# An attention and gated FFN kernel: content products of queries and keys on row halves, the norm's steps and products on other engines, pools in another order

## The chip, the cores and the metric

One core of a Trainium2 chip. The time is the device time of one execution in microseconds (us), the median of several runs; smaller is better. TensorE (PE) multiplies matrices, VectorE (DVE), ScalarE (ACT) and GpSimd (POOL) work elementwise, and SyncE (SP) issues the DMAs.

## The reference

Everything is fp32. For x of 8 batches, 256 positions and 512 columns, with 128 heads of 4 content columns and 64 rotary columns:

```python
xn = (x - mean(x)) / sqrt(var(x) + 1e-5)
c_q, c_kv = xn @ Wq_down, xn @ Wkv_down              # 512 -> 64 each
q_c, k_c, v_c = c_q @ Wq_up, c_kv @ Wk_up, c_kv @ Wv_up   # 64 -> 128 heads x 4
q_r, k_r = xn @ Wq_rope, xn @ Wk_rope                # 128 heads x 64; one of 64 for all heads
scores = (q_c . k_c + q_r . k_r) / sqrt(68)
s = softmax(scores) @ v_c @ Wo
lin(x, wq, A, B) = x @ tile(wq, 4).T + 0.5 * x @ A.T @ B.T
g = silu(lin2(silu(lin1(xn)) * lin3(xn)))            # 512 -> 1376 -> 512, rank 2
out = x + s * g
```

## The kernel before

**First phase** (`first_phase`, the first 230 us or so). The 2048 rows are four blocks (`tb`) of 512 rows, each of four x tiles of 128 rows. For a block, `norm` takes mean and variance of the four tiles on DVE (L359, L360), adds the epsilon (L365) and makes a first guess of the reciprocal root by integer operations (L368, L370); `norm_rest` refines it in three Newton steps of three small DVE operations (L377, L378, L380) and scales the four tiles (L385). `turn` transposes the tiles on TensorE (xpt, L401), copies them out on ACT and DVE in turn (L404, L406) and sums column chunks for the FFN (L410 to L412). `narrow` (pm) and `down` (pp) are the narrow products: `narrow` gives the rank-2 inputs and the rotary keys, `down` the two latents, 64 rows of queries' and 64 of keys'. `down` also calls `sum_x`, which makes sums of x chunks on POOL (L158) and stores them. Then six steps `u` of the FFN follow: `low` (px and py, L451) and `main` (L463, L464), with silu on ACT (L466) and the product hT on DVE (L468, L471, L472), `fold` on POOL (L486 to L488) and `low_out` (pm, L498) on TensorE. `gate_out` (pf) makes the gate of a block, which is stored to DRAM (L524, L525). The work of the next block is set among these steps by hand: its `norm` at u = 1, its `norm_rest` at u = 2, its `turn` after u = 5. `between` sets other work there: `set_up`, which lays out the weights of the content products by POOL copies, and in the last block the first pieces of the second phase.

**Second phase.** 64 blocks `n` are pairs of a batch `b` and a group of 16 heads `sg`; each is done in two halves. A half issues two `score` groups on TensorE (sc, L672, tiles of 32 rows by 128 columns), the maxima on DVE (nmx, L685), exponentials on ACT (pr, L691), transposes on DVE (pt, L701), and one `Project`: the rotary queries of a later block by seven products in place of eight (q, L173, tiles of 128 rows by 32 columns), for which weights w come from DRAM (L124) and their sums ws from POOL (L136 to L139) or DRAM. In a block's first half come also `weigh` (av, L718, the weighted values of the block before), `gather` (L738), and every other pair of blocks `prepare`: the content queries and keys of 32 heads for one batch (qk, 32 calls in all). The stationary weights there are `wupq_sb`, whose lower 64 rows are zero, and `wupk_sb`, whose upper 64 rows are zero, so that each product over all 128 rows of the latents takes its own half. Eight PSUM banks, handed out in rotation by `bank`, carry all of this.

After the first phase its pools are closed, and `w2p` (for `wo_sb`), `prp`, `tp`, `smp` and `op` are opened where they lay. SP's queue then holds, in this order, the gates' stores, the latents of two batches (`load_act`), 32 loads of Wo (L649) and the loads of w. At the end `give` multiplies the output product by the gate, adds x and stores it.

Each engine works off its own instructions in the order in which the program issues them, and so does the queue of SP.

Of the kernel before, what the change touches and what calls it, by code (L numbers as in the profile page):

```python
# [9 lines left out]
F32 = mybir.dt.float32  # L10
I32 = mybir.dt.int32
AF = mybir.ActivationFunctionType
ALU = mybir.AluOpType
# [3 lines left out]
P = 128  # L17
# [7 lines left out]
TB = 512  # L25
# [12 lines left out]
def mla_ffn_gate_kernel(  # L38
# [25 lines left out]
    const = pool("const", 1)  # L64
    ident = const.tile([P, P], F32, name="ident")
    make_identity(nc, ident)
    wupq_sb = const.tile([P, 4, P], F32, name="wupq_sb")
    wupk_sb = const.tile([P, 4, P], F32, name="wupk_sb")
    wv_sb = const.tile([P, 4, P], F32, name="wv_sb")
    mask_sb = const.tile([P, 8], F32, name="mask_sb")  # L70

# [27 lines left out]
    def bank(name):  # L99
        return ps_all.tile([P, 512], F32, tag="b", name=name)  # L100
# [68 lines left out]
    def on_columns(to, w, x, start, stop):  # L169

        for t in range(4):
            tile_ = slice(32 * t, 32 * t + 32)
            nc.tensor.matmul(to[tile_], w[:, tile_], x, start=start, stop=stop, skip_group_check=True)  # L173
# [65 lines left out]
    def prepare(b, g):  # L239


        qk = bank(f"qk_{b}_{g}")
        on_columns(qk[:, :S], wupq_sb[:, g, :], acts[b][:, 0, :], True, True)
        on_columns(qk[:, S:], wupk_sb[:, g, :], acts[b][:, 0, :], True, True)
        qc = qcp.tile([P, S], F32, tag="qc", name=f"qc_{b}_{g}", bufs=3)
        nc.scalar.copy(qc, qk[:, :S])  # L246
        kc = qcp.tile([P, S], F32, tag="kc", name=f"kc_{b}_{g}", bufs=3)
        nc.scalar.mul(kc, qk[:, S:], QSCALE)
        qks[b, g] = qc, kc

    def spread(n):
# [37 lines left out]
    def first_phase(between):  # L289
# [63 lines left out]
        load_x(1)  # L353

        def norm(tb):
            mv = f2.tile([P, 4, 2], F32, tag="mv", name=f"mv_{tb}")
            for n in range(4):
                s6 = f2.tile([P, 6], F32, tag="st", name=f"st_{tb}_{n}")
                nc.vector.bn_stats(s6, xts[tb][n])  # L359
                nc.vector.bn_aggr(mv[:, n, :], s6)  # L360


            var = mv[:, :, 1]
            ve = f2.tile([P, 4], F32, tag="ve", name=f"ve_{tb}")
            nc.vector.scalar_tensor_tensor(ve, var, EPS, var, ALU.add, ALU.max)  # L365

            i0 = f2.tile([P, 4], I32, tag="i0", name=f"i0_{tb}")
            nc.vector.tensor_single_scalar(i0, ve.bitcast(I32), 1, ALU.logical_shift_right)  # L368
            r0 = f2.tile([P, 4], I32, tag="r0", name=f"r0_{tb}")
            nc.vector.tensor_scalar(r0, i0, -1.0, float(0x5F3759DF), ALU.mult, ALU.add)  # L370
            r0 = r0.bitcast(F32)
            return mv, ve, r0

        def norm_rest(tb, mv, ve, r0):
            e = f2.tile([P, 4], F32, tag="e", name=f"e_{tb}")
            for step in range(3):
                nc.vector.scalar_tensor_tensor(e, r0, -0.5, r0, ALU.mult, ALU.mult)  # L377
                nc.vector.scalar_tensor_tensor(e, e, 1.0, ve, ALU.mult, ALU.mult)  # L378
                rstd = f2.tile([P, 4], F32, tag="rstd", name=f"rstd_{tb}_{step}")
                nc.vector.scalar_tensor_tensor(rstd, e, 1.5, r0, ALU.add, ALU.mult)  # L380
                r0 = rstd
            xns[tb] = []
            for n in range(4):
                xn = xts[tb][n]
                nc.vector.scalar_tensor_tensor(  # L385
                    xn,
                    xn,
                    mv[:, n, 0:1],
                    rstd[:, n : n + 1].to_broadcast([P, D]),
                    ALU.subtract,  # L390
                    ALU.mult,
                )
                xns[tb].append(xn)

        def turn(tb):
            a = f1.tile([P, KT, TB], F32, tag="act1", name=f"act1_{tb}")
# [17 lines left out]

        def over_xn(tb, name, weights):
            ps = bank(f"{name}_{tb}")
            for c in range(KT):
                on_columns(ps, weights[:, c, :], xnT[tb][:, c, :], c == 0, c == KT - 1)
            return ps

        def narrow(tb):
# [116 lines left out]
        for tb in range(NTB):  # L538
            more = tb + 1 < NTB
            for u in range(6):  # L540
                low(tb, u)
                main(tb, u)
                if u in (2, 4):
                    fold(tb, u // 2 - 1)
                    low_out(tb, u // 2 - 1)
                if u == 1 and more:
                    stats = norm(tb + 1)
                if u == 2 and more:
                    norm_rest(tb + 1, *stats)
                if u == 1 and tb + 2 < NTB:  # L550
                    load_x(tb + 2)
                if tb == NTB - 2 and u == 1:
                    between(1)
                if u == 5:
                    fold(tb, 2)
                if not more:
                    between(u + 2)
            if more:
                turn(tb + 1)
                low_out(tb, 2)  # L560
                narrow(tb + 1)
                down(tb + 1)
            else:
                low_out(tb, 2)
            gate_out(tb)
# [5 lines left out]
    def set_up():  # L571
# [5 lines left out]
        nc.sync.dma_start(out=v_raw[64:128, :], in_=w_v)  # L577
        for t in range(4):
            nc.sync.dma_start(out=mask_sb[32 * t : 32 * t + 32, :], in_=kmask[0:32, :])
        nc.gpsimd.memset(wupq_sb[64:128], 0.0)  # L580
        nc.gpsimd.memset(wupk_sb[0:64], 0.0)
        nc.gpsimd.memset(wv_sb[0:64], 0.0)
        up = up_raw.rearrange(
            "l (g h u z j i d) -> l g h u z j i d", g=4, h=2, u=2, z=2, i=2, d=HD
# [2 lines left out]
        for r in range(4):  # L587
            for h in range(2):
                to = slice(32 * r + 16 * h, 32 * r + 16 * h + 16)
                of = up[:, :, h, r % 2, 0, :, r // 2, :]  # L590
                for w_sb, rows in ((wupq_sb, slice(0, 64)), (wupk_sb, slice(64, 128))):
                    nc.gpsimd.tensor_copy(
                        w_sb[rows, :, to].rearrange("l g (j d) -> l g j d", d=HD), of[rows]
                    )
            for t in range(4):
                nc.gpsimd.tensor_copy(
                    wv_sb[64:128, t, :].rearrange("l (s r d) -> l s r d", s=8, d=HD)[:, :, r],
                    vr[64:128, :, r % 2, t, r // 2, :],
                )
# [38 lines left out]
    first_phase(between)  # L638


    w2p = pool("wo", 1)
    wo_sb = w2p.tile([P, KT, D], F32, name="wo_sb")

    wo = w_o.rearrange("(c e u t i d) m -> e u t i d c m", e=2, u=2, t=4, i=2, d=HD)
    for r in range(4):
        for t in range(4):
            for e in range(2):
                p = 32 * r + 8 * t + 4 * e
                nc.sync.dma_start(out=wo_sb[p : p + 4], in_=wo[e, r % 2, t, r // 2])  # L649
    prp = pool("pr", 6)  # L650
    tp = pool("pt", 3)
    smp = pool("sm", 2)
    op = pool("out", 2)
    scs, nmxs, prs, pts, accs, outT = {}, {}, {}, {}, {}, {}

    def score(n, f):
# [125 lines left out]
                pos[b, n], outT[b][:, c, ds(n * P, P)], wo_sb[:, c, :], c == 0, c == KT - 1  # L782
            )

    def give(b, n, engine=nc.gpsimd):
        g, xr = gxs.pop((b, n))
        nc.vector.tensor_mul(g, pos[b, n], g)
        engine.tensor_add(g, g, xr)
        nc.sync.dma_start(out=out[ds(b * S + n * P, P), :], in_=g)

    def finish(b, n):
        put(b, n, range(KT))
# [90 lines left out]
    put(B - 1, 1, range(KT))  # L883
    for b in (B - 2, B - 1):
        for i in range(2):
            give(b, i, nc.vector if (b, i) == (B - 1, 1) else nc.gpsimd)


# [64 lines left out]
```

## Time and profile before

| | |
|---|---|
| median of 3 runs | 2027.2 us (2026.76 to 2027.53) |
| profiled execution | 2026.23 us, its span 2024.5 us |
| granted TensorE clock, mean | 0.999 |
| busy: TensorE, DVE, ACT, POOL | 99%, 76%, 53%, 36% of the span |
| HBM read and written | 145.12 MB and 34.08 MB |

A row of a timeline gives the start in us, the length in us, the engine, the line of the kernel, the operation with its output and inputs by the program's names, the shapes, the count, and in brackets how long the engine stood idle before it and what released it. Rows of one kind that follow each other are merged. PEld is TensorE's loading of weights, SPq the queue of SyncE. A row of the waits gives who waited for whom, the sum in us, how often, and the longest. The ends of TensorE's records are modelled, so starts are what is compared here. One fp32 product leaves two records.

### The profile page before, as it was taken

What the parts mean: (1) busy time and instruction counts of PE and PEld (TensorE: products, weight loads), DVE (VectorE), ACT (ScalarE), POOL (GpSimd) and SP (SyncE); (2) the same over time, 40 slices, a digit from 0 to 9 for tenths busy, and PEclk for the clock granted to TensorE, in tenths of its full rate; (3) what the DMA queues carried; (4) which work ended last, traced back from release to release, by engine and by line L of the source; (5) the groups of instructions that cost most, each with busy time, mean ns of one, the idle gap of its engine ahead of it and who ended that gap; (6) DMA issues with size and microseconds to landing.
All of it is one profiled execution on the core that took longest, in us unless ns stands there. A gap on an engine that the chain in (4) does not pass through costs nothing.

```text
span 2024.5 us, 86560 instructions
## 1 busy us (share of the span) xinstructions
PE 2008.1 (99%) x38080; PEld 1417.0 (70%) x38080; DVE 1544.5 (76%) x2638; ACT 1072.4 (53%) x2978; POOL 720.7 (36%) x1044
## 2 busy tenths in 40 slices
PE   8999999999999999999999999999999999999998
PEld 3334477777777776777777777677777767777776
DVE  6542387878798777878787877878787877888788
ACT  1222365565556554556555644555555545556654
POOL 5434445545552323233232233223323223232231
PEclk9999999999999999999999999999999999999999
DMA  5233322222223223322223123222223222222212
GB/s 167 87 113 134 110 97 75 76 86 86 86 75 128 80 91 103 99 86 67 84 86 122 65 105 110 81 82 86 68 90 115 82 100 81 86 85 79 72 55 70
DMA packets 118043, 184.77 MB, mean 91 GB/s; under 512 B 10434, under 2 KB 83810, under 8 KB 117668
## 3 DMA queue, kind: packets, MB, share of 16 engines
q1 hardware_dynamic: 117668, 179.23, 26.0%
q8 instruction: 301, 4.93, 1.0%
q14 instruction: 74, 0.61, 0.1%
HBM read 145.12 MB, written 34.08 MB: 89 GB/s over the span
## 4 chain that ended last, share of the span: by engine, by line
PE 95%; DVE 1%; DMA 0%; issue 0%; ACT 0%; POOL 0%; SPq 0%; DVEq 0%; ACTq 0%
PE q L173 39%; PE sc L672 33%; PE av L718 11%; PE po L173 2%; PE pf L173 2%; PE px L173 2%; PE py L173 1%; PE qk L173 1%; PE px L451 1%; PE vps L270 1%; DVE pt L701 1%; PE pm L173 1%; PE pp L173 1%; PE pm L498 0%; DVE nmx L685 0%
## 5 line engine op out<-in xcount | busy, mean ns | idle before, releaser
L691 ACT ACTIVATE pr<-sc,nmx 128x256 f32<-128x256 f32 x2048 | 816.4, 502 | 476.4 <-DVE nmx L685 470.9
L685 DVE TENSOR_REDUCE nmx<-sc 128x2 f32<-128x512 f32 x1024 | 635.4, 683 | 318.8 <-PE sc L672 293.3
L701 DVE STREAM_TRANSPOSE pt<-pr 128x512 f32<-128x512 f32 x1024 | 634.8, 677 | 0.0
L672 PE MATMUL sc<-act,qr 32*128 32x256 f32 x8192 | 490.1, 374 | 0.1
L173 PE MATMUL q<-x,ws 128*32 128x256 f32 x8192 | 488.8, 379 | 0.1
L216 POOL TENSOR_TENSOR e<-e,e 128x256 f32<-128x256 f32 x128 | 94.0, 734 | 1059.0 <-ACT e L211 557.1
L672 PEld LDWEIGHTS sc<-act,qr 32*128 32x128 f32 x8192 | 422.6, 185 | 21.9 <-issue 0.3
L173 PEld LDWEIGHTS q<-x,ws 128*32 128x32 f32 x8192 | 265.0, 110 | 177.4 <-POOL ws L137 0.6
L173 PE MATMUL q<-x,w 128*32 128x256 f32 x6144 | 381.5, 381 | 1.4 <-ACT pr L691 1.4
L173 PEld LDWEIGHTS q<-x,w 128*32 128x32 f32 x6144 | 186.4, 110 | 155.5 <-ACT pr L691 40.9
L672 PE MATMUL sc<-kc,qcm 32*128 32x256 f32 x4096 | 281.9, 387 | 0.0
L718 PE MATMUL av<-pt,vpad 128*32 128x128 f32 x8192 | 236.4, 273 | 1.9 <-ACT pr L691 1.2
L718 PEld LDWEIGHTS av<-pt,vpad 128*32 128x32 f32 x8192 | 226.3, 110 | 14.5 <-issue 3.0
L672 PEld LDWEIGHTS sc<-kc,qcm 32*128 32x128 f32 x4096 | 199.1, 184 | 52.1 <-issue 38.4
L211 ACT COPY e<-q 128x256 f32<-128x256 f32 x512 | 203.9, 399 | 14.9 <-PE q L173 14.7
L738 ACT ACTIVATE acc<-av,sides_sb 128x256 f32<-128x256 f32 (+1 forms) x130 | 54.2, 468 | 219.2 <-PE av L718 219.2
L255 POOL TENSOR_TENSOR qcm<-qc,mask_sb 128x1024 f32<-128x1024 f32 x64 | 122.2, 1910 | 9.1 <-ACT qc L246 9.1
L217 POOL TENSOR_TENSOR e<-e,e 128x256 f32<-128x256 f32 x128 | 93.6, 731 | 10.0
L218 POOL TENSOR_TENSOR qr<-e,e 128x256 f32<-128x256 f32 x128 | 93.6, 731 | 10.0
L285 POOL COPY vpad<-vall 32x128 f32<-32x128 f32 x256 | 74.8, 292 | 16.0 <-ACT vall L277 5.6
L228 DVE TENSOR_TENSOR qr<-e,q 128x256 f32<-128x256 f32 x128 | 53.9, 421 | 26.2 <-PE q L173 13.6
L468 DVE TENSOR_TENSOR hT<-gate,py 128x512 f32<-128x512 f32 x32 | 21.3, 684 | 65.9 <-PE py L173 39.6
(103 smaller groups left out, 1114.3 us busy)
## 6 DMA issues: line engine op xcount, KB each, us to landing
w<-in_w_rope_dram SPq DMA_DIRECT2D x128, 512.0 KB
ws<-sums_d SPq DMA_DIRECT2D x96, 512.0 KB
sums_d<-ws SPq DMA_DIRECT2D x32, 512.0 KB
x<-xs_d SPq DMA_DIRECT2D x28, 256.0 KB
xt<-in_x_dram SPq DMA_DIRECT2D x16, 256.0 KB
xs_d<-xt SPq DMA_DIRECT2D x16, 256.0 KB
gate_d<-gs SPq DMA_DIRECT2D x16, 256.0 KB
g<-gate_d SPq DMA_DIRECT2D x16, 256.0 KB
```

Of the source, the lines that this page charges most:

```text
L173: nc.tensor.matmul(to[tile_], w[:, tile_], x, start=start, stop=stop, skip_group_check=True)
L211: nc.scalar.copy(self.e[i], self.banks[i])
L216: nc.gpsimd.tensor_add(m6, m6, m1)
L217: nc.gpsimd.tensor_add(m7, m7, m6)
L218: nc.gpsimd.tensor_add(self.out(1, 1), self.split(m7), self.split(m5))
L255: nc.gpsimd.tensor_mul(qcm, qks[b, sg // 2][0].rearrange("p (q i) -> p q i", i=32).unsqueeze(2).to_broadcast([P, 8, 4, 32]), mask_sb[:, ds ...
L285: nc.gpsimd.tensor_copy(vpad[rows, :, :, 8 * t + 4 * (sg % 2) :][..., :4], valls[b][rows, :, sg])
L672: nc.tensor.matmul(sc[r][:, h, :], lhs.rearrange("p t i -> p (t i)"), rhs, start=(part == 0 and h == 0), stop=(part == 2), skip_group_chec ...
L685: nc.vector.tensor_reduce(nmx[:, r, :], scs[n, f][r], AX.X, ALU.max, negate=True)
L691: nc.scalar.activation(p[:, h, :], scs[n, f][r][:, h, :], AF.Exp, bias=nmxs[n, f][:, r, h : h + 1])
L701: nc.vector.transpose(pts[n, f // 2, r].rearrange("p k q i -> p q k i")[:, ds(2 * (f % 2), 2)], prs.pop((n, f, r)).rearrange("p h (k j) -> ...
L718: nc.tensor.matmul(av[32 * r : 32 * r + 32, ds(half * P, P)], vpad[:, k, r, :], pt[r][:, k].rearrange("p q i -> p (q i)"), start=(k == 0), ...
```

## The change

`prepare` multiplies only the 64 rows that matter: the queries' rows 0 to 63 and the keys' rows 64 to 127, each from its own half of one weights tile `wup_sb`, in turn and into two banks. `set_up` fills that tile with half the copies and without zeroing. In `norm` the Newton steps now stand at u = 1; for block 0 they stay on DVE, for the others they run on POOL, which also makes the offset, minus mean times reciprocal root. `norm_rest` stands at u = 4; for block 0 it scales on DVE by `tensor_scalar`, for the others on ACT by one activation per tile. The first `narrow` product of block 0 is made in two halves of its columns. `prp`, `smp` and `op` are opened ahead of `w2p`. The last `give` works in two halves of the columns.

```diff
--- before.py
+++ after.py
@@ -64,8 +64,7 @@
     const = pool("const", 1)
     ident = const.tile([P, P], F32, name="ident")
     make_identity(nc, ident)
-    wupq_sb = const.tile([P, 4, P], F32, name="wupq_sb")
-    wupk_sb = const.tile([P, 4, P], F32, name="wupk_sb")
+    wup_sb = const.tile([P, 4, P], F32, name="wup_sb")
     wv_sb = const.tile([P, 4, P], F32, name="wv_sb")
     mask_sb = const.tile([P, 8], F32, name="mask_sb")
 
@@ -239,13 +238,18 @@
     def prepare(b, g):
 
 
-        qk = bank(f"qk_{b}_{g}")
-        on_columns(qk[:, :S], wupq_sb[:, g, :], acts[b][:, 0, :], True, True)
-        on_columns(qk[:, S:], wupk_sb[:, g, :], acts[b][:, 0, :], True, True)
+        qk = [bank(f"q{'qk'[k]}_{b}_{g}")[:, :S] for k in range(2)]
+        for t in range(4):
+            to = slice(32 * t, 32 * t + 32)
+            for k in range(2):
+                rows = slice(64 * k, 64 * k + 64)
+                nc.tensor.matmul(
+                    qk[k][to], wup_sb[rows, g, to], acts[b][rows, 0, :], start=True, stop=True
+                )
         qc = qcp.tile([P, S], F32, tag="qc", name=f"qc_{b}_{g}", bufs=3)
-        nc.scalar.copy(qc, qk[:, :S])
+        nc.scalar.copy(qc, qk[0])
         kc = qcp.tile([P, S], F32, tag="kc", name=f"kc_{b}_{g}", bufs=3)
-        nc.scalar.mul(kc, qk[:, S:], QSCALE)
+        nc.scalar.mul(kc, qk[1], QSCALE)
         qks[b, g] = qc, kc
 
     def spread(n):
@@ -353,44 +357,48 @@
         load_x(1)
 
         def norm(tb):
+
+
             mv = f2.tile([P, 4, 2], F32, tag="mv", name=f"mv_{tb}")
             for n in range(4):
                 s6 = f2.tile([P, 6], F32, tag="st", name=f"st_{tb}_{n}")
                 nc.vector.bn_stats(s6, xts[tb][n])
                 nc.vector.bn_aggr(mv[:, n, :], s6)
-
-
-            var = mv[:, :, 1]
             ve = f2.tile([P, 4], F32, tag="ve", name=f"ve_{tb}")
-            nc.vector.scalar_tensor_tensor(ve, var, EPS, var, ALU.add, ALU.max)
-
+            nc.vector.tensor_scalar_add(ve, mv[:, :, 1], EPS)
             i0 = f2.tile([P, 4], I32, tag="i0", name=f"i0_{tb}")
             nc.vector.tensor_single_scalar(i0, ve.bitcast(I32), 1, ALU.logical_shift_right)
             r0 = f2.tile([P, 4], I32, tag="r0", name=f"r0_{tb}")
             nc.vector.tensor_scalar(r0, i0, -1.0, float(0x5F3759DF), ALU.mult, ALU.add)
-            r0 = r0.bitcast(F32)
-            return mv, ve, r0
-
-        def norm_rest(tb, mv, ve, r0):
+            r = r0.bitcast(F32)
             e = f2.tile([P, 4], F32, tag="e", name=f"e_{tb}")
             for step in range(3):
-                nc.vector.scalar_tensor_tensor(e, r0, -0.5, r0, ALU.mult, ALU.mult)
-                nc.vector.scalar_tensor_tensor(e, e, 1.0, ve, ALU.mult, ALU.mult)
-                rstd = f2.tile([P, 4], F32, tag="rstd", name=f"rstd_{tb}_{step}")
-                nc.vector.scalar_tensor_tensor(rstd, e, 1.5, r0, ALU.add, ALU.mult)
-                r0 = rstd
-            xns[tb] = []
-            for n in range(4):
-                xn = xts[tb][n]
-                nc.vector.scalar_tensor_tensor(
-                    xn,
-                    xn,
-                    mv[:, n, 0:1],
-                    rstd[:, n : n + 1].to_broadcast([P, D]),
-                    ALU.subtract,
-                    ALU.mult,
-                )
-                xns[tb].append(xn)
+                new = f2.tile([P, 4], F32, tag=f"r{step}", name=f"r_{tb}_{step}")
+                if tb == 0:
+                    nc.vector.scalar_tensor_tensor(e, r, -0.5, r, ALU.mult, ALU.mult)
+                    nc.vector.scalar_tensor_tensor(e, e, 1.0, ve, ALU.mult, ALU.mult)
+                    nc.vector.scalar_tensor_tensor(new, e, 1.5, r, ALU.add, ALU.mult)
+                else:
+                    nc.gpsimd.tensor_mul(e, r, r)
+                    nc.gpsimd.tensor_mul(e, e, ve)
+                    nc.gpsimd.tensor_scalar(e, e, -0.5, 1.5, ALU.mult, ALU.add)
+                    nc.gpsimd.tensor_mul(new, e, r)
+                r = new
+
+            off = f2.tile([P, 4], F32, tag="off", name=f"off_{tb}")
+            if tb:
+                nc.gpsimd.tensor_mul(off, mv[:, :, 0], r)
+                nc.gpsimd.tensor_scalar(off, off, -1.0, None, ALU.mult)
+            return mv, r, off
+
+        def norm_rest(tb, mv, rstd, off):
+            xns[tb] = xts[tb]
+            for n, xn in enumerate(xts[tb]):
+                one = rstd[:, n : n + 1]
+                if tb:
+                    nc.scalar.activation(xn, xn, AF.Identity, bias=off[:, n : n + 1], scale=one)
+                else:
+                    nc.vector.tensor_scalar(xn, xn, mv[:, n, 0:1], one, ALU.subtract, ALU.mult)
 
         def turn(tb):
             a = f1.tile([P, KT, TB], F32, tag="act1", name=f"act1_{tb}")
@@ -414,8 +422,11 @@
 
         def over_xn(tb, name, weights):
             ps = bank(f"{name}_{tb}")
-            for c in range(KT):
-                on_columns(ps, weights[:, c, :], xnT[tb][:, c, :], c == 0, c == KT - 1)
+            for cols in (ds(0, S), ds(S, S)) if name == "pm" and tb == 0 else (ds(0, TB),):
+                for c in range(KT):
+                    on_columns(
+                        ps[:, cols], weights[:, c, :], xnT[tb][:, c, cols], c == 0, c == KT - 1
+                    )
             return ps
 
         def narrow(tb):
@@ -545,7 +556,7 @@
                     low_out(tb, u // 2 - 1)
                 if u == 1 and more:
                     stats = norm(tb + 1)
-                if u == 2 and more:
+                if u == 4 and more:
                     norm_rest(tb + 1, *stats)
                 if u == 1 and tb + 2 < NTB:
                     load_x(tb + 2)
@@ -577,8 +588,6 @@
         nc.sync.dma_start(out=v_raw[64:128, :], in_=w_v)
         for t in range(4):
             nc.sync.dma_start(out=mask_sb[32 * t : 32 * t + 32, :], in_=kmask[0:32, :])
-        nc.gpsimd.memset(wupq_sb[64:128], 0.0)
-        nc.gpsimd.memset(wupk_sb[0:64], 0.0)
         nc.gpsimd.memset(wv_sb[0:64], 0.0)
         up = up_raw.rearrange(
             "l (g h u z j i d) -> l g h u z j i d", g=4, h=2, u=2, z=2, i=2, d=HD
@@ -588,10 +597,7 @@
             for h in range(2):
                 to = slice(32 * r + 16 * h, 32 * r + 16 * h + 16)
                 of = up[:, :, h, r % 2, 0, :, r // 2, :]
-                for w_sb, rows in ((wupq_sb, slice(0, 64)), (wupk_sb, slice(64, 128))):
-                    nc.gpsimd.tensor_copy(
-                        w_sb[rows, :, to].rearrange("l g (j d) -> l g j d", d=HD), of[rows]
-                    )
+                nc.gpsimd.tensor_copy(wup_sb[:, :, to].rearrange("l g (j d) -> l g j d", d=HD), of)
             for t in range(4):
                 nc.gpsimd.tensor_copy(
                     wv_sb[64:128, t, :].rearrange("l (s r d) -> l s r d", s=8, d=HD)[:, :, r],
@@ -638,6 +644,9 @@
     first_phase(between)
 
 
+    prp = pool("pr", 6)
+    smp = pool("sm", 2)
+    op = pool("out", 2)
     w2p = pool("wo", 1)
     wo_sb = w2p.tile([P, KT, D], F32, name="wo_sb")
 
@@ -647,10 +656,7 @@
             for e in range(2):
                 p = 32 * r + 8 * t + 4 * e
                 nc.sync.dma_start(out=wo_sb[p : p + 4], in_=wo[e, r % 2, t, r // 2])
-    prp = pool("pr", 6)
     tp = pool("pt", 3)
-    smp = pool("sm", 2)
-    op = pool("out", 2)
     scs, nmxs, prs, pts, accs, outT = {}, {}, {}, {}, {}, {}
 
     def score(n, f):
@@ -782,11 +788,13 @@
                 pos[b, n], outT[b][:, c, ds(n * P, P)], wo_sb[:, c, :], c == 0, c == KT - 1
             )
 
-    def give(b, n, engine=nc.gpsimd):
+    def give(b, n, engine=nc.gpsimd, parts=1):
         g, xr = gxs.pop((b, n))
-        nc.vector.tensor_mul(g, pos[b, n], g)
-        engine.tensor_add(g, g, xr)
-        nc.sync.dma_start(out=out[ds(b * S + n * P, P), :], in_=g)
+        for i in range(parts):
+            cols = ds(i * (D // parts), D // parts)
+            nc.vector.tensor_mul(g[:, cols], pos[b, n][:, cols], g[:, cols])
+            engine.tensor_add(g[:, cols], g[:, cols], xr[:, cols])
+            nc.sync.dma_start(out=out[ds(b * S + n * P, P), cols], in_=g[:, cols])
 
     def finish(b, n):
         put(b, n, range(KT))
@@ -883,7 +891,10 @@
     put(B - 1, 1, range(KT))
     for b in (B - 2, B - 1):
         for i in range(2):
-            give(b, i, nc.vector if (b, i) == (B - 1, 1) else nc.gpsimd)
+            if (b, i) == (B - 1, 1):
+                give(b, i, nc.vector, 2)
+            else:
+                give(b, i)
 
 
 # ---- launch: one core; the weights laid out for it, inputs and outputs in their types ----
```

## The prediction

> **What bounds the kernel.** I read the page first: the shares of busy time, the forty slices, then the chain that ended last.
>
> ```profile
> span 2024.5 us, 86560 instructions
> PE 2008.1 (99%) x38080; PEld 1417.0 (70%) x38080; DVE 1544.5 (76%) x2638; ACT 1072.4 (53%) x2978; POOL 720.7 (36%) x1044
> ...
> PE 95%; DVE 1%; DMA 0%; issue 0%; ACT 0%; POOL 0%; SPq 0%; DVEq 0%; ACTq 0%
> PE q L173 39%; PE sc L672 33%; PE av L718 11%; PE po L173 2%; PE pf L173 2%; PE px L173 2%; PE py L173 1%; PE qk L173 1%; PE px L451 1%; PE vps L270 1%; DVE pt L701 1%; PE pm L173 1%; PE pp L173 1%; PE pm L498 0%; DVE nmx L685 0%
> ```
>
> TensorE is the chain. So a change is worth what it does to TensorE's issue, or to the few places where TensorE stands still. A fp32 product leaves two records, so record counts below are twice the matmuls. The timeline of TensorE around one `prepare` shows the pace:
>
> ```profile
> 301.16 1.91 PE L173 MATMUL q<-x,w 128*32 128x256 f32 x32
> 302.89 1.05 PE L173 MATMUL q<-x,ws 128*32 128x256 f32 x16
> 303.75 0.61 PE L173 MATMUL qk<-act,wupq_sb 128*32 128x256 f32 x8
> 304.18 0.61 PE L173 MATMUL qk<-act,wupk_sb 128*32 128x256 f32 x8
> 304.61 3.68 PE L718 MATMUL av<-pt,vpad 128*32 128x128 f32 x128
> 308.22 1.15 PE L672 MATMUL sc<-kc,qcm 32*128 32x256 f32 x16
> ...
> 311.78 1.91 PE L672 MATMUL sc<-act,qr 32*128 32x256 f32 x32
> 313.61 1.07 PE L173 MATMUL q<-x,w 128*32 128x256 f32 x16
> ```
>
> From start to start: 16 records of q take 0.86 us, 54 ns each; qk the same, so one `prepare` costs 0.86 us, 32 of them 27.6 us; 128 records of av, half as wide, take 3.61 us, 27 ns each plus 0.15. Where the shape of the tiles changes (32 sc records at 54 ns from 311.78 end at 313.51, q starts at 313.61) 0.10 to 0.11 us are lost. Over the loop a group of 112 q records costs 0.13 us above its pace when sc follows and 0.02 when qk or av follows; so 0.11 is the price of a change of shape. A sc group costs 0.21 above its pace, 0.11 of it on leaving.
>
> Then the waits and the timeline of the first phase (first 230 us), the only long stretch with holes:
>
> ```profile
> PE xpt L401 <- DVE xt L385: 3.0, 1, 3.0
> PE pm L498 <- DVE hT L468: 2.7, 1, 2.7
> ...
> PE q L173 <- ACT pr L691: 1.4, 1, 1.4
> ```
> ```profile
> 39.91 1.21 DVE L377 SCALAR_TENSOR_TENSOR e<-rstd 128x4 f32<-128x4 f32 x1
> 46.22 3.71 DVE L385 SCALAR_TENSOR_TENSOR xt<-xt,mv,rstd 128x512 f32<-128x512 f32 x4
> 49.85 1.27 DVE L468 TENSOR_TENSOR hT<-gate,py 128x512 f32<-128x512 f32 x2
> ```
> ```profile
> 46.86 1.03 PE L498 MATMUL pm<-hT,a_sb 128*32 128x512 f32 x4
> 50.58 1.64 PE L498 MATMUL pm<-hT,a_sb 128*32 128x512 f32 x4 [2.69 <-DVE hT L468]
> 52.15 0.69 PE L451 MATMUL px<-mid,b_sb 2*128 2x512 f32 x1
> ```
>
> In block 0 the Newton steps for block 1 run on DVE while POOL does `sum_x`; steps of 0.16 us take up to 1.21. DVE is through with steps and products at 49.9, hT is late, and TensorE's pm2 group takes 5.29 us from 46.86 to 52.15 where block 1 takes 0.97 (89.29 to 90.26): **4.3 us lost**. Blocks 1 and 2 show no such hole.
>
> **What the Trainium skill says.** "TensorEngine Tiling (Array Packing)", Key Properties: a change of tiling mode drains TensorE, and tiles of one mode run in parallel; 64x32 has eight tiles. The trace agrees on the drain (0.11 us) and shows four tiles in parallel, never eight. "TensorE: Matmul & The Clock Gate", LDWEIGHTS: time goes by columns over 1.2 GHz, so 32 columns are an estimated 27 ns; av's 27 ns per pair of load and product shows that this rate can be kept. "VectorE: DVE Perf Modes", the perf-mode tier table: a fp32 `tensor_scalar` from SBUF runs at two elements a cycle, 1227 ns for 2048; by that table 512 elements are an estimated 0.43 us, against 0.69 for L385 undisturbed. No row of before shows it. "GPSIMD Engine Reference", Specifications: POOL shares SBUF interfaces with DVE instructions that have two SBUF inputs; the 0.16 against 1.21 us above agrees.
>
> **Part by part.**
>
> *prepare.* Eight products of 128x32 with half of the rows zero become eight of 64x32, in two banks. If eight tiles overlap, 16 records go at 27 ns: 0.43 us. Two changes of shape are added, since q stands before and av after: 0.11 to enter, 0.13 to leave (the last record now ends further behind its successor's slot, 27 ns more), and 0.02 to 0.13 to fill the array. Sum 0.67 to 0.80; I take 0.73. Against 0.86 that gains 0.13 us, times 30 in the loop, 3.9 us. The two in the first phase run together and a change of shape follows them anyway: 1.73 becomes 0.11 + 0.86 + 0.06, gain 0.7. **Together -4.6** (bounds: -6.5, and +11.5 if nothing overlaps). The added bank moves the rotation of the eight by one; the banks it takes are those of sc `two`, whose exponentials end more than 1 us before; cost nothing, covered by the second products of `Project`. With that cover gone a wait would show as q or sc on ACT pr. The copies qc and kc keep size and engine.
>
> *Norm of blocks 1 to 3.* From DVE go 9 steps and 4 products per block; to POOL come 14 small operations (COPY 128x8 there takes 0.19 us; bounds 0.1 to 0.3 each: 1.4 to 4.2 us, I take 2.8), to ACT four of 128x512 at 0.6 us (the gate of that size is 597 ns): 2.4. The POOL chain stands after `sum_x(0)`, which ends at 42.3 and, with eight copies of 0.27 less in `set_up`, some 2 us earlier; so it is done by 43. Behind it waits `fold(0)`, wanted only by pf at 65. ACT's products come after the gates of u = 4 and end by about 48.5, xpt then starts at about 50.7 less what the start gains; behind them waits the gate of the last chunk, whose px is not there before 49. Hidden. Identity beside Silu may load tables: nothing for COPY in the trace; at worst 1.28 us (the load shown) twice a block, on an ACT that is idle over three quarters. So the hole closes: **-4.3** (bounds -4.5 and -1). Blocks 1 and 2: nothing.
>
> *Start.* In block 0 products take 0.43 instead of 0.69, so the first transpose starts 0.26 earlier. TensorE paces the transposes itself (0.86 us for one x tile, the clock granted is low there: 0.66 from 10 to 15 us), ending at 14.6. pm waited until 15.90 for the last DVE copy; its first half of the columns needs only tiles 0 and 1 and may start at 14.75, a quarter of a microsecond of it at low clock. The second half, about 1.8 us later, finds its copies. **-1.0** (bounds -0.2, if the wait is still for all four copies, and -1.6). The added records (32) cost nothing at 54 for 107 ns.
>
> *Pools.* Before, the first maxima of the loop wait for the gate's store, and TensorE stands 1.35 us at 247.51:
>
> ```profile
> DVE nmx L685 <- DMA gate_d<-gs: 12.4, 1, 12.4
> ```
> ```profile
> 247.51 1.07 PE L173 MATMUL q<-x,w 128*32 128x256 f32 x16 [1.35 <-ACT pr L691]
> ...
> 264.99 0.55 SPq L124 DMA_DIRECT2D w<-in_w_rope_dram  x1
> ...
> 271.90 2.31 PEld L173 LDWEIGHTS q<-x,ws 128*32 128x32 f32 x48 [0.56 <-POOL ws L137]
> ```
>
> That wait goes. But late next is ws: the load of w for the third half stands on SP's queue behind ten act loads and 32 of Wo, and is issued at 264.99 whatever DVE does; TensorE already waits about 0.3 us for it and would then wait 1.6. The queue's order is unchanged, so I take **0** (bounds 0 and -1.4).
>
> *End and set_up.* The last product, sum and store are halved: by the 691 ns of 512 elements, two halves cost DVE more, not less, and the last store is half as large. -0.1 (bounds -0.4, +0.4). Fewer and larger copies in `set_up`: POOL alone, 2 us, off the chain.
>
> **Sum**: -4.6 - 4.3 - 1.0 - 0.1 = -10.0. The profiled execution took 2026.23 (span 2024.5 and 1.7 around it), so 2016.2; the median of the three runs lies 1.0 above the profiled one, so **2017.2**.
>
> **Rivals.**
>
> *A. Overlap is eaten by the drains.* Only the price of leaving 128x32 and 32x128 is shown; if 64x32 fills as sc does or worse, `prepare` stays at 0.86. Left: norm, start and end, -5.4: 2021.8. For it: only two records per tile, so fill weighs most. Chance 0.15.
>
> *B. The hole moves instead of closing.* xpt of block 1 waits for ACT or the POOL chain (14 operations in sequence at 0.3 or more), or the gates wait behind ACT's products. It would give back up to 4.3: 2021.5. Against it: about 2 us of room above. Chance 0.08.
>
> *C. Slower: row halves do not overlap.* Place: each `prepare`. If the eight tiles go at the 54 ns of four, it takes 0.86 + 0.36 = 1.22 instead of 0.86, +0.36 times 32 = +11.5, less 5.4: +6, 2033. It decides above about 48 ns a record (the gain of the rest, 5.4, over 32 leaves 0.17 above 0.86; less 0.27 of drains, 0.76 over 16). For it: no row of before has tiles split both ways with different moving data; against it: sc overlaps row groups, q overlaps columns. Chance 0.12.
>
> *D. The change does as costed, 2017.2*: 0.65. A measurement of this kernel can tell about 0.2%, 4 us, from no change. D, nearly all of A and B are faster: 0.84. A with B, and a mild C, lie within: 0.06. C: 0.10.
>
> **Range.** From D with its good bounds (prepare -6.5, pools -1.4, start -1.6: about 2012.5) to A and B with a little more loss: 2023.5. C lies outside.
>
> **What would show it.** qk records of 64x32 about 27 ns apart, and 0.73 us from the first qk record to av plus drain before it (right); 54 ns apart (C). pm L498 on hT gone from the waits, 0.97 us for that group, and no xpt wait on ACT (B). pm's first record near 14.8. At the loop's start no wait of nmx on the gate's store, but a longer one of q on ws. The forecast is wrong if sc or q groups of the loop change their 5.39 and 6.18 us, or a bank wait appears after `prepare`.

## The result, and the profile after

The kernel after takes **2018.06 us** (median, 2016.41 to 2019.40); the kernel before, beside it, took 2027.37 (2025.79 to 2029.15). The ratio is 0.9954, with a 95% interval of 0.9941 to 0.9967. The profiled execution took 2017.04 us where that of before took 2026.23: 9.19 less, and its span is 9.2 shorter. The forecast was 2017.2, so the total was right to 1 us. Its parts were not: the two large gains came as costed where they were looked for, but both were given back in part elsewhere, and a gain came where none was expected.

From the page of the kernel after, the span, the row of TensorE and the chain that ended last:

```profile
span 2015.3 us, 86608 instructions
...
PE 2006.2 (100%) x38112; PEld 1406.4 (70%) x38112; DVE 1523.0 (76%) x2601; ACT 1081.8 (54%) x2990; POOL 727.7 (36%) x1076
...
PE 98%; DVE 2%; issue 0%; DMA 0%; SPq 0%; DVEq 0%
```

TensorE was 95% of the chain and is 98%: ACT and POOL have left it, and the kernel is bound as before. The timeline of TensorE around one `prepare`, in the kernel after (of the sixteen content records, four are shown):

```profile
296.17 1.05 PE L172 MATMUL q<-x,ws 128*32 128x256 f32 x16
297.14 0.40 PE L246 MATMUL qq<-act,wup_sb 64*32 64x256 f32 x1
...
297.19 0.40 PE L246 MATMUL qk<-act,wup_sb 64*32 64x256 f32 x1
...
297.38 0.38 PE L246 MATMUL qq<-act,wup_sb 64*32 64x256 f32 x1
...
297.43 0.38 PE L246 MATMUL qk<-act,wup_sb 64*32 64x256 f32 x1
...
297.74 3.70 PE L724 MATMUL av<-pt,vpad 128*32 128x128 f32 x128
301.37 1.15 PE L678 MATMUL sc<-kc,qcm 32*128 32x256 f32 x16
```

Eight records, four tiles of queries and four of keys, start within 0.05 us; the other eight, the second pass of each fp32 product, follow 0.24 later. So eight tiles do overlap. From the first content record to av it is 0.60 us, where two groups took 0.86. The q records in front of it took 0.86 and take 0.97 now: that is the price of entering.

To see where the 9.2 us come from, I cut both traces of TensorE at the same instructions and compared the stretches:

| stretch on TensorE | before | after | difference |
|---|---|---|---|
| span's start to the first px | 22.91 | 19.25 | -3.66 |
| block 0, u = 0 and 1: that px to the first L498/L509 pm | 13.81 | 16.88 | +3.07 |
| block 0, rest: to xpt of block 1 | 18.35 | 14.02 | -4.33 |
| block 1: xpt to xpt | 48.24 | 49.33 | +1.09 |
| block 2: xpt to xpt | 48.23 | 48.22 | -0.01 |
| block 3: xpt to the first sc | 89.16 | 88.07 | -1.09 |
| loop's start: first sc to first av | 36.41 | 34.61 | -1.80 |
| loop: first av to last av | 1733.94 | 1731.57 | -2.37 |
| last av to the end of the span | 13.45 | 13.35 | -0.10 |
| sum | 2024.5 | 2015.3 | -9.20 |

**The hole of block 0.** The waits of TensorE in the kernel after hold one of the three rows that were shown for before, that of xpt:

```profile
PE av L724 <- ACT pr L697: 1.2, 1, 1.2
PE xpt L409 <- DVE xt L401: 0.6, 1, 0.6
```

Neither the wait of pm on hT nor that of q on pr is left. The row of xpt belongs to the start: it is the first transpose of block 0, which waits 0.6 instead of 3.0 us. The 1.2 of av on pr is one place of the loop and was there before. The timelines of POOL, TensorE and DVE in that stretch, in the kernel after:

```profile
40.45 0.21 POOL L382 TENSOR_TENSOR e<-r 128x4 f32<-128x4 f32 x1
...
44.12 0.23 POOL L391 TENSOR_SCALAR off<-off 128x4 f32<-128x4 f32 x1
44.32 1.29 POOL L497 TENSOR_TENSOR h<-hT 128x512 f32<-128x512 f32 x1
```
```profile
46.26 1.04 PE L509 MATMUL pm<-hT,a_sb 128*32 128x512 f32 x8
47.23 0.69 PE L462 MATMUL px<-mid,b_sb 2*128 2x512 f32 x1
```
```profile
46.91 0.68 DVE L482 TENSOR_TENSOR hT<-gate,py 96x512 f32<-96x512 f32 x1 [4.28 <-POOL h4b L498]
```

pm to px is 0.97 us, where it was 5.29. But look at the last row. DVE stands 4.28 us in front of a product of u = 4, for POOL's `fold`, which starts only when the Newton steps (40.45 to 44.32) are through. TensorE doesn't feel that wait in this execution: from xpt to pp of block 1 it is 6.53 us, as before. In other kernels with the same norm it does (below).

**The start.** From the timelines of TensorE and DVE in the kernel after:

```profile
10.17 2.03 PE L409 MATMUL xpt<-ident,xt 128*128 128x128 f32 x16 [0.58 <-DVE xt L401]
12.23 3.66 PE L172 MATMUL pm<-act,ck_sb 128*32 128x256 f32 x64
```
```profile
28.42 0.16 DVE L606 TENSOR_REDUCE sides_sb<-mask_sb 128x2 f32<-128x8 f32 x1 [11.72 <-DMA mask_sb<-in_kmask_dram]
28.52 2.70 DVE L479 TENSOR_TENSOR hT<-gate,py 128x512 f32<-128x512 f32 x4
```

pm starts at 12.23 instead of 15.90. Most of this is not the change's: the sixteen transposes went at full clock in this execution, 2.03 us, and at a low one in that of before, 3.58. And what is gained meets a wait at a fixed time: DVE's sum of the mask, in `set_up`, waits until the mask has landed at 28.4, and the products hT stand behind it. These products free py's banks, so TensorE stands some 1.4 us, and after that stop the granted clock is about 0.5 from 31.0 to 34.4 us, so that eight px records take 1.94 us there and 1.04 elsewhere. Of 3.66 us, 0.59 remain.

### The profile page after: what moved, and what is told of

Its sections match the earlier page's. It is cut to its first block, busy times and chain, and to the rows that moved or that the text cites. A ratio compares the mean times of both kernels' runs of the same rounds, so it can differ in the third digit from the quotient of the medians.

```text
span 2015.3 us, 86608 instructions
## 1 busy us (share of the span) xinstructions
PE 2006.2 (100%) x38112; PEld 1406.4 (70%) x38112; DVE 1523.0 (76%) x2601; ACT 1081.8 (54%) x2990; POOL 727.7 (36%) x1076
## 4 chain that ended last, share of the span: by engine, by line
PE 98%; DVE 2%; issue 0%; DMA 0%; SPq 0%; DVEq 0%
PE q L172 39%; PE sc L678 34%; PE av L724 11%; PE po L172 2%; PE px L172 2%; PE pf L172 2%; PE py L172 2%; PE px L462 1%; PE qq L246 1%; PE pm L172 1%; PE vps L274 1%; PE pp L172 1%; DVE pt L707 1%; PE pm L509 0%; DVE nmx L691 0%; PE xpt L409 0%
```

## The experiments

Times are medians, and each ratio is to the kernel before on the same chip. On the first of these chips the kernel before ran at 2025.5 us but from 2020.3 to 2031.9, so medians alone would not have settled parts of 1 to 4 us; the stretches of the table above, read from each trace, do.

**prepare alone** (prep_only): the kernel before with the new `prepare` and its weights tile.

```diff
+        qk = [bank(f"q{'qk'[k]}_{b}_{g}")[:, :S] for k in range(2)]
...
+                    qk[k][to], wup_sb[rows, g, to], acts[b][rows, 0, :], start=True, stop=True
```

> The kernel before with only the new prepare and its weights tile. Theory (overlap with two added drains, as costed): q groups ahead of it grow from 6.07 to 6.18 us, the group of 16 records takes 0.60, av grows by 0.02: -0.13 each in the loop and -0.7 for the two of the first phase, -4.7 us in all, 2022.6. Rival (the added bank makes the score groups after it or the q groups wait for exponentials, as the scattered late q starts of the changed kernel suggest): about 1.5 us of that is lost, -3.2, and the waits of q on ACT pr grow against before. Rival (no overlap of row halves): slower, +8 or more.

2023.91 us, ratio 0.999 [0.9981, 1.0]. At each of the 30 places of the loop the group takes 0.59 to 0.60 us, the q group ahead of it 6.18 (6.07 before) and av behind it 3.63 (3.61): -0.13 each, -3.9 in all. In the first phase the two calls gave 0.7. The span of the profile is 3.1 us shorter, but 1.6 of that lie at the start, which the edit doesn't touch, and the loop is only 0.36 us shorter. Two things ate the rest of the 3.9. From a first sc to the next q it is 5.39 us as a rule; what goes beyond that, called late q below, sums to 4.57 us in 10 places, where before had 1.68 in 5; and once sc waits 0.70 us for ACT's `acc`. The late ones look like this on TensorE's weight loads, in the kernel prep_only:

```profile
1424.74 0.30 PEld L671 LDWEIGHTS sc<-kc,qcm 32*128 32x128 f32 x5 [0.20 <-issue]
1425.58 0.51 PEld L671 LDWEIGHTS sc<-kc,qcm 32*128 32x128 f32 x9 [0.54 <-issue]
```

Within one sc group the loads pause for 0.54 us, and they wait for nothing that the timeline shows. The price of a call is settled, then, and the loss of some 3 us beside it is seen but not explained. But one thing goes with it, the queue that brings instructions. The page of prep_only gives its packets, megabytes and share:

```profile
q8 instruction: 301, 4.93, 1.0%
```

The second load above begins 2.46 us after a transfer of that queue began. In the twelve profiles there are 35 late sc groups in which TensorE falls behind by more than 0.25 us at one step, and all 35 steps come 1.9 to 3.2 us after the start of such a transfer, though these are 6.6 us apart on the mean. Most transfers pass without a pause, and that they cause the pauses is not shown. Nor is it shown whether the new `prepare`, which changes the run of instructions and takes a bank more, adds to them: the three kernels with the old one have 1.7, 1.5 and 3.1 us of late q, the nine with the new one 2.6 to 4.8.

**The norm alone** (norm_only): the kernel before with `norm` and `norm_rest` of blocks 1 to 3 as in the change; block 0 keeps its old products.

```diff
-                if u == 2 and more:
+                if u == 4 and more:
                     norm_rest(tb + 1, *stats)
```

> The kernel before with only the norm of blocks 1 to 3 changed: Newton steps on POOL, products on ACT at u = 4; block 0 scales as before. Theory: the hole of 4.3 us at pm in block 0 closes, and POOL's 14 small operations (0.28 us from start to start, 3.9 us) make sum_x and its stores later, so the gate's stores on SP's queue come later and a gate waits for a gs buffer in block 1, +1.1: net -3.2, 2024.0. Rival: the late gate stores belong to the earlier start and not to POOL; then net -4.3, 2022.9. Rival: the hole moves to xpt: 0 to -1.

2022.81 us, ratio 0.998 [0.9972, 0.9989]. The hole is closed to the hundredth, 18.35 to 14.02, but block 1 takes 51.59 instead of 48.24 us: 3.35 of 4.33 are given back. The waits of this kernel from 49 to 101 us, and TensorE's timeline at the turn:

```profile
DVE hT L477 <- POOL h4b L493: 8.1, 1, 8.1
```
```profile
55.84 3.64 PE L173 MATMUL pm<-act,ck_sb 128*32 128x512 f32 x32 [0.37 <-DVE act L412]
```

DVE loses 8.1 us in front of hT of u = 4, so it comes late to the copies of `turn`, and the narrow products of block 1 wait for it: from xpt to pp it is 9.74 us, where it was 6.53. The reason is a buffer. hT has two buffers for the pieces that `fold` adds, so the product of u = 4 takes the place of a piece that `fold(0)` must first have read; and `fold(0)` stands on POOL behind `set_up`, `sum_x` and now the Newton steps. The expectation had the loss smaller, +1.1, and at another place, the gate's stores.

That second place shows in the kernel after. There xpt to pp is 6.53 us as before, and all of the 1.09 are lost behind pp, where ACT's third copy of the gate waits for the store that frees its buffer. The row of before, then that of after:

```profile
76.26 1.23 ACT L524 ACTIVATE gs<-pf 128x512 f32<-128x512 f32 x2 [1.78 <-DMA gate_d<-gs]
75.04 1.21 ACT L535 ACTIVATE gs<-pf 128x512 f32<-128x512 f32 x2 [5.48 <-DMA gate_d<-gs]
```

That store is late by way of three queues. The folds make POOL late with its sum of x chunks in `turn`, so DVE waits longer for it and makes `mid` later. On SP's queue the store of `mid` stands ahead of those of the sums, and these ahead of the gate's. SP issues the gate's first store 2.06 us after its copy has started, where it was 0.62. DVE's wait, before and after:

```profile
DVE xs L412 <- POOL xs L411: 2.4, 1, 2.4
DVE xs L420 <- POOL xs L419: 3.8, 1, 3.8
```

**The pools alone** (pools_only): `prp`, `smp` and `op` ahead of `w2p`, in the kernel before.

```diff
+    prp = pool("pr", 6)
+    smp = pool("sm", 2)
+    op = pool("out", 2)
     w2p = pool("wo", 1)
```

> The kernel before with only prp, smp and op opened ahead of w2p. Theory: the first maxima no longer wait for the gate's store, TensorE's hole of 1.4 us at the start of the loop goes, and the wait for ws of about 0.3 us goes too because SP's queue reaches the load of w earlier: -1.8, 2025.4. Rival (as forecast): the load of w comes no earlier, the time gained is waited for ws: 0, 2027.2, with a wait of q on POOL ws of 1.6 us.

2028.39 us, ratio 1.0012 [1.0002, 1.0021]: no gain. The wait on the gate's store is gone; from the first sc to q it is 5.39 instead of 6.81 us. But 24 us later, on TensorE's timeline of pools_only:

```profile
270.35 1.07 PE L173 MATMUL q<-x,w 128*32 128x256 f32 x16 [1.06 <-DMA w<-in_w_rope_dram]
272.06 2.80 PE L173 MATMUL q<-x,ws 128*32 128x256 f32 x48 [0.63 <-POOL ws L137]
```

1.69 us, against the 1.6 that the prediction worked out. SP issues that load of w at 264.89, in before at 264.99: the queue sets it, as the prediction had it. First sc to first av is 36.58, before 36.41.

**Order of the row halves** (rows_apart): the kernel after, with the two loops of `prepare` exchanged, so that the four query tiles come first and then the four of keys.

```diff
-        for t in range(4):
-            to = slice(32 * t, 32 * t + 32)
-            for k in range(2):
-                rows = slice(64 * k, 64 * k + 64)
+        for k in range(2):
+            rows = slice(64 * k, 64 * k + 64)
+            for t in range(4):
+                to = slice(32 * t, 32 * t + 32)
```

> The changed kernel with the two loops of prepare exchanged: four products of the queries' rows, then four of the keys' rows. Theory (row halves overlap only if they are issued in turn, since products start in order): the second half can start only when the second pass of the first half has started, so 0.2 us are added to each group of 0.60 us and prepare is no cheaper than before. Rival (the order doesn't matter, the engine overlaps across it): 0.60 us again, 2017.

2021.13 us in one execution. The groups again take 0.59 to 0.60 us, and the keys' products start 0.02 us behind the queries':

```profile
299.78 0.42 PE L246 MATMUL qq<-act,wup_sb 64*32 64x256 f32 x4
299.80 0.42 PE L246 MATMUL qk<-act,wup_sb 64*32 64x256 f32 x4
```

So the theory was wrong. The alternating order buys nothing; that the halves of the rows are separate tiles is enough.

**The mask's sum later** (after_sides): the reduction into `sides_sb` goes from `set_up` into `between`, at u = 1 of block 2.

```diff
-        nc.vector.tensor_reduce(
-            sides_sb, mask_sb.rearrange("p (n e) -> p e n", e=2), AX.X, ALU.add
-        )
...
         elif step == 1:
+            nc.vector.tensor_reduce(
+                sides_sb, mask_sb.rearrange("p (n e) -> p e n", e=2), AX.X, ALU.add
+            )
```

> The changed kernel with one thing moved: the small reduction that makes sides_sb from the mask is issued in block 2 instead of in set_up. Theory: in the changed kernel DVE waits there for the mask until 28.4 us with hT queued behind it, px banks come free late, TensorE stands still and its clock goes down; without it the lead of 3.7 us that the start had at 23 us is kept: -2.5 to -3 us against the changed kernel, about 2015.3. Rival: something else is late next (w2 or the sums of block 1, x of block 1), and less than 1 us is kept. Rival: only the idle time goes, not the low clock: -1.4.

2019.38 us, ratio 0.9966 [0.9955, 0.9976]: not the 2015.3 that were expected, and by its ratio no faster than the kernel after. The profile can't answer by itself: px starts at 21.56 here, and with so late a start u = 0 and 1 take 13.81 whether the sum was moved or not (rows_apart, 21.58, 13.81). The three kernels below that contain this edit and start early, gates_first, best and setup_late with px at 19.78, 20.05 and 19.96, have 13.81 to 13.82. Their first products hT, in gates_first at 22.92, 24.63 and 27.56, run before 28.4, when DVE of the kernel after was still standing. So the loss of 3.07 belongs to that wait, and it only shows when the start is fast. This rests on three profiles against one.

**prepare behind the values** (after_late): the kernel after, with `prepare` called after `place_values`, so that its 64x32 group stands between av and sc instead of between q and av.

```diff
-                if n + 2 <= last and blocks[n + 2][1] % 2 == 0:
-                    prepare(blocks[n + 2][0], blocks[n + 2][1] // 2)
...
                     place_values(n)
...
+                if n + 2 <= last and blocks[n + 2][1] % 2 == 0:
+                    prepare(blocks[n + 2][0], blocks[n + 2][1] // 2)
```

> The changed kernel with prepare called after weigh, gather and place_values, so that on TensorE it stands between av and sc, where the shape of the tiles changes anyway. Theory (each change of shape costs about 0.11 us and the leaving of 64x32 a little more): one change of shape is saved at each of 30 places, -0.11 to -0.14 each, -3.3 to -4.2 us, about 2014.3. Rival (what is paid is the filling of eight tiles, not the change): nothing, 2018. Rival (slower): qc and kc come some 4 us later, spread and the scores that need them wait, +2 or more.

2014.32 us, ratio 0.9937 [0.992, 0.9953]; beside it on the chip after_sides took 2019.38. On TensorE's timeline of after_late:

```profile
298.34 3.67 PE L724 MATMUL av<-pt,vpad 128*32 128x128 f32 x128
301.94 0.40 PE L246 MATMUL qq<-act,wup_sb 64*32 64x256 f32 x1
...
302.53 1.15 PE L678 MATMUL sc<-kc,qcm 32*128 32x256 f32 x16
```

q and av have the same shape of tiles, av and sc do not. Moved there, the group replaces one change of shape by two where it had replaced none by two. The q records are back at 0.87 us, av takes 3.60, and the group 0.59. The loop goes from 1731.57 to 1726.82 us, -4.75, of which 30 times 0.13 are 3.9; of the rest, 0.5 is fewer late q.

**The gates ahead of the sums** (gates_first): on top of after_sides, POOL's `sum_x` of the next block comes after `gate_out` instead of in `down`, so that the sums' stores no longer stand ahead of the gate's on SP's queue.

```diff
             gate_out(tb)
+            if more:
+                sum_x(tb + 1, xnT[tb + 1])
```

> As the kernel with the moved reduction, and sum_x of the next block is issued after gate_out, so that the gates' stores stand ahead of its stores on SP's queue. Theory (in the changed kernel the gates' stores wait behind stores that wait for POOL): ACT's wait for a gs buffer in block 1 falls from 5.5 us to about 2 and TensorE's loss of 1.1 us there goes: about 1.1 us below the kernel with the moved reduction. Rival: the stores themselves take that long to land and the wait stays: no change.

2016.82 us, ratio 0.9952 [0.9935, 0.9968]. SP issues the gate's first store 0.62 us after its copy has started, as before the change. ACT's third copy waits 3.23 us (5.85 in after_sides), and from pp to xpt of block 2 it is 41.71 us, as in before (43.17 in after_sides). But block 1 still takes 49.57 us: DVE waits 6.22 for POOL's h4b, and xpt to pp is 7.86. Two causes, then, and this removes one.

**The three together** (best): after_sides, after_late and gates_first in one kernel.

> The three edits together: reduction moved, gates' stores first, prepare between av and sc. Theory: they add up, -2.7 - 1.1 - 3.7 = -7.5 against the changed kernel, about 2010.5. Rival: the earlier start meets a wait of the loop's start (the load of w behind the loads of Wo) and only prepare's part remains: about 2014.

2012.56 us, ratio 0.9928 [0.9912, 0.9945]. The loop is at 1726.55; block 1 is at 50.41, with DVE's wait at 7.0 us. DVE comes to the buffer at 40.4 us here and came at 42.6 in the kernel after, so the lead that the start now keeps is in part spent on waiting for POOL: 2 us of the 7.5 are missing.

**POOL's room** (setup_late): on top of after_sides, POOL's copies of `set_up` move to u = 2 of block 1, and the zeroing of the values' padding to u = 2 of block 2.

```diff
+                if u == 2 and tb == 1:
+                    set_up_copies()
+                if u == 2 and tb == 2:
+                    set_up_vpads()
```

> The kernel with the moved reduction, and POOL's part of set_up (copies and memsets) moved out of block 0 into blocks 1 and 2. Theory (the Newton steps on POOL stand ahead of fold(0), fold(0) frees the hT buffer that the products of u = 4 need, so DVE is late into turn): in block 0 POOL is then ahead, DVE's wait for POOL h4b of 4 to 8 us goes, pm of block 1 starts 3.1 us after its xpt as before the change instead of 3.8 to 6.3, and from xpt to xpt of block 1 it takes 48.3 to 49.3 us instead of the 50.4 of the kernel with the moved reduction: -1 to -2 us against it. Rival (the loss in block 1 belongs to the gates' stores alone): pm stays as late, no gain. Rival: the copies delay fold in block 1 and the wait comes there.

2015.44 us, ratio 0.9937 [0.992, 0.9955]. DVE's timeline of setup_late has, at the product that waited:

```profile
42.57 0.68 DVE L482 TENSOR_TENSOR hT<-gate,py 96x512 f32<-96x512 f32 x1 [2.29 <-PE py L172]
```

It waits for TensorE's py, no longer for POOL. xpt to pp is 6.53 and block 1 48.25, as before the change; block 2 takes 48.93, +0.7, where work was put. So the loss of block 1 is POOL's lateness, and not the place of ACT's products, which are the same here. ACT's third copy of the gate still waits 3.4 us, and that costs nothing.

Block 1 in before and in all kernels with the new norm, in us:

| kernel | DVE's wait for h4b | xpt to pp | ACT's wait, third copy of the gate | pp to xpt of block 2 |
|---|---|---|---|---|
| before | none | 6.53 | 1.78 | 41.71 |
| after | 4.28 | 6.53 | 5.48 | 42.80 |
| rows_apart | 4.96 | 6.60 | 5.96 | 44.98 |
| after_sides | 5.57 | 7.21 | 5.85 | 43.17 |
| after_late | 5.91 | 7.55 | 5.81 | 43.13 |
| gates_first | 6.22 | 7.86 | 3.23 | 41.71 |
| best | 7.05 | 8.69 | 3.26 | 41.71 |
| norm_only | 8.09 | 9.74 | 4.43 | 41.85 |
| setup_late | none | 6.53 | 3.39 | 41.71 |
| best2 | none | 6.53 | 3.13 | 41.71 |

The first 4.9 us of DVE's wait cost TensorE nothing, and what goes beyond them comes back whole in xpt to pp. Of ACT's wait some 4.4 us are free in the same way. Only rows_apart loses 1.7 us more in the last column; its granted clock was 0.5 there from 77.2 to 80.6 us.

**All four** (best2):

> All edits: prepare between av and sc, reduction moved, gates' stores first, POOL's part of set_up moved. Theory: both causes of the loss in block 1 are gone, so from xpt of block 1 to that of block 2 it takes the 48.24 us of the kernel before instead of 50.4: about -2 against the kernel with the first three edits, 2010.5. Rival: the w load at the loop's start, which comes when SP's queue lets it, takes it back: 2012.5.

**2011.59 us** (2008.52 to 2012.70), ratio 0.9915 [0.9899, 0.9932]. Blocks 1 and 2 take 48.24 and 48.22. This beats both kernels. The loop is 1728.42 us, with 4.4 of late q against 2.6 in best, whose code is the same there: this unexplained loss is worth about as much as the smaller edits.

## Why the prediction was right

By its own terms (-10.0 in all, -9.2 in the profile):

- **prepare, -4.6.** Size and mechanism hold: 0.60 for the group, 0.11 to enter and 0.02 on av make 0.73, the value taken. -3.9 in the loop and -0.7 in the first phase were measured. Rival A (0.86) and rival C (1.22) fall. Not foreseen: the loop of the kernel after gave 2.37 of the 3.9, since late q rose from 1.7 to 3.3 us. TensorE's waits have no new one on ACT pr, which was the sign named for a missing bank.
- **Norm, -4.3: the failed step.** The hole gave 4.33. But "Behind it waits fold(0), wanted only by pf at 65" was wrong, and with it "Blocks 1 and 2: nothing". pf is the reader of the folded sums; a buffer also waits for the reader of what it held. hT of u = 4 wants the buffer that `fold(0)` frees, 17 us earlier than pf in the kernel after and 21 in norm_only. And what stands further behind on POOL was not followed at all: its sum in `turn`, and through that the gate's stores. In the kernel after the first wait stayed within its room of 4.9 us and the second cost 1.09; in norm_only the first cost 3.2 of the 3.35. So the term is -3.2 here and -1.0 in norm_only, at the upper bound. Rival B was this in kind, a hole that moves, but it looked for it at xpt of block 1, or at gates that wait behind ACT's products and not for their own stores. The POOL chain took 3.9 us, 0.28 from start to start fourteen times, not 2.8; the bound was 4.2. ACT's four products took 2.92, not 2.4.
- **Start, -1.0.** The mechanism holds: pm starts after its first half's copies. Its size has to be read between executions with the same clock. From xpt to px, prep_only and norm_only, with the old start, took 10.52 and 10.53 us at full clock, and the four kernels with the new start at full clock 9.08: -1.4. With half clock for a while, before and pools_only took 11.46 and 11.37, four with the new start 10.53 to 10.59: -0.9. So the term was right. In the two profiles the difference was -3.66, and 3.07 of it returned at the mask, a wait that the prediction did not have: it asked what is late next for the loop, but not for the start.
- **Pools, 0.** Right alone, as pools_only shows. With the rest it isn't: in the eight kernels that hold the whole change, first sc to first av is 34.61 to 35.73 us, 0.7 to 1.8 less than before. The kernel after has the lowest, since q waits there neither for w nor for ws; in the others 0.5 to 1.1 us of such waits are left. SP's queue runs further ahead of the first sc: the load of w is issued 22.44 us after it instead of 24.29. Of these 1.85 us, the gates' stores give 1.0 (3.94 us instead of 4.91), the second batch's and Wo's loads 0.9. "The queue's order is unchanged" was true, its timing was not. Why the stores go faster I didn't pursue.
- **End, -0.1.** -0.10. DVE's halves take 0.42 each instead of 0.69, so two cost more, and the smaller last store makes up for it.

In sum, the terms that missed (+1.5 in the loop, +1.1 in block 1, +0.4 at the start, -1.8 at the loop's start, -0.4 more in block 3) nearly cancel. The total was right partly by luck; the 0.8 us left between forecast and profile say nothing of the parts.

## What to carry to other kernels

When work moves to another engine, follow everything queued behind it there, and for each item ask not only who reads its result but whose buffer it frees: the nearest of the two is its due time. A group of another tile shape belongs at a place where the shape changes anyway; here that was worth as much as the halved group itself, 3.9 us each. And a gain at one place must be followed to the next event that stands at a fixed time, a landed load or a queue of loads, since it ends there.

## What the runs showed of the hardware

- Eight 64x32 tiles, four on each half of the rows with different moving data, start within 0.05 us, and the passes of the fp32 products follow 0.24 us apart (the Trainium skill, "TensorEngine Tiling (Array Packing)", Key Properties, says that tiles of one mode run in parallel; the trace agrees, for eight).
- Four DVE products of 128x512 in fp32 from SBUF by `tensor_scalar` take 1.92 us and start 0.46 apart, against the estimate of 0.43 from the Trainium skill, "VectorE: DVE Perf Modes", the perf-mode tier table; the measured value decides. On ACT the same four, each one activation with scale and bias, take 2.92 us and start 0.71 apart.
- POOL's operations on 128x4 elements take 0.20 us and start 0.28 apart, though each has four elements to a row.
- In six of the twelve profiles TensorE stood 2.1 to 3.0 us before its first transpose, and the granted clock was 0.5 for 3.4 us, from 10.9 to 12.4 us on; in the other six it stood 0.6 to 1.9 us and the clock stayed full. The sixteen transposes took 2.5 to 3.6 us in the first six and 2.0 to 2.6 in the others. Later and shorter stops went either way: 1.4 us at 29 us in the kernel after were followed by 3.4 us at half clock, as much in block 1 of after_sides and after_late was not.
- Pauses in sc groups behind av or `prepare` cost 1.5 to 4.8 us in each profile, at mostly the same places in several kernels. The large ones go with transfers of instructions, 1.9 to 3.2 us after the start of one; what causes them stays open.
